# Attention and 7x7 involution on one core: shifted copies become a ring of padded rows, products take 3 or 4 taps, units begin with their own rows, the last two chunks go in half blocks

## The chip, the cores and the metric

The kernel runs on one core of a Trainium2 chip. The metric is the device time of one execution in microseconds (us); less is better. The core has five engines that each work through a queue of their own: TensorE (PE in the profile; its weight loads are shown as PEld), VectorE (DVE), ScalarE (ACT), GpSimd (POOL) and SyncE (SP), which here only issues DMA transfers. They meet through semaphores: an instruction at the head of a queue waits until its semaphores have the value that it needs, and everything behind it in that queue waits too.

## The reference

Everything is float32. `x` is 4 images of 512 channels and 64 x 64 pixels. Layer 0 is self-attention over the 4096 pixels of an image with 128 inner channels; layer 1 is a bottleneck whose middle is an involution: each pixel makes its own 7 x 7 weights for 8 groups of 16 channels.

```python
def _L0_conv_ref(x, wq, bq, wk, bk, wv, bv, wo, bo):
    ...
    q = jnp.einsum('oc,bcn->bon', wq, xf) + bq[:, None]
    k = jnp.einsum('oc,bcn->bon', wk, xf) + bk[:, None]
    v = jnp.einsum('oc,bcn->bon', wv, xf) + bv[:, None]
    energy = jnp.einsum('bci,bcj->bij', q, k)
    attn = jax.nn.softmax(energy, axis=-1)
    out = jnp.einsum('bcj,bij->bci', v, attn)
    out = jnp.einsum('oc,bcn->bon', wo, out) + bo[:, None]
    out = out.reshape(b, c, h, w) + x
    return out
...
def involution(x, Wr, sr, br, Ws, bs):
    w = jax.nn.relu(affine(conv1x1(x, Wr), sr, br))
    w = conv1x1(w, Ws) + bs[None, :, None, None]
    w = w.reshape(B, G, K * K, H, W)
    ...
    out = jnp.einsum('bgkhw,bgckhw->bgchw', w, patches)
    return out.reshape(B, C, H, W)
out = jax.nn.relu(affine(conv1x1(x, W1), s1, b1))
out = involution(out, Wr, sr, br, Ws, bs)
out = affine(conv1x1(out, W3), s3, b3)
return out + x
```

## The kernel before

The whole work is in `fast_path`. (A slower general path follows it, and is entered only if the softmax sums left a safe range; here it is not.) An image is 8 chunks of 512 pixels, a chunk is 8 image rows, and a *unit* of the involution is 4 rows, so 256 pixels: partitions hold 128 pixels, and two such tiles make a unit. An image has 16 units.

*Main line.* For each image `keys_values` (L335) computes the keys `k` and the transposed values `v` chunk by chunk, and `attention` (L481) then runs 32 steps for each chunk of queries. A step is: a score matmul `pss` (128 keys x 512 queries, into one of two PSUM buffers with the tag `s`, L493), an exp on ScalarE into `pt` (L496, five buffers), a matmul `po` with the values (L517), and on VectorE the running sum of the exps `pacc` (L520, L522, at the end `sums`, L525). The score of step m+2 is written ahead of the `po` of step m. Only the last chunk of the last image goes in two half blocks of 256 queries, with 32 steps each.

*Side work.* After each step `chores` (L210) advances three lists of Python generators by a little, so that their instructions fall between those of the main line; the scheduler then sets the final order within each engine's queue. `finish_block` (L388) takes a chunk from the softmax division to layer 1's input: the sum over partitions `pl` (L405), reciprocals (L411), `on` (L414), the projection `pwo` (L418) with the residual (L420), the bottleneck `p1` (L428), its transposed pixels into a padded DRAM image `pix` (L456), and the reduced channels `red` (L465). `close_chunk` (L319) computes the last projection `py` with the residual and writes the output. `pace` (L180) lets the involution go on by 0.78 products for each planned us of TensorE.

*Involution.* A unit is released (L470) when the rows that it needs, three of the next chunk among them, are there. `pump` (L188) then loads its shifted copies from `pix` by four DMA transfers (L204): for 4 and for 3 horizontal shifts, 9 rows each, 1152 and 864 KB, into the pools `sa` (two buffers) and `sb` (one). `weights` (L216) makes the per-pixel weights `pw` of the unit in PSUM, a tile of two banks with a pool tag of its own (L218). `involution` (L230) issues the products: VectorE multiplies two vertical taps at a time, 128 x 512 (L264; 24 of them a unit, and one of a single tap), reading `copies` from SBUF and `pw` from PSUM; POOL adds each product into `acc` (L285) and folds `acc` at the end (L294). There are seven product buffers. `turn_unit` (L298) transposes the sum (`pa`, L308).

*Tail.* After the last image's attention (loop at L542) the units that are left are finished: every second product is then summed by TensorE into `accp` (L279) instead of by POOL, and VectorE adds that sum into `acc` (L293).

PSUM is eight banks of 512 float32 columns a partition. Before, they are: tag `mm` 2, tag `s` 2, `w` (the `pw` tile) 2, `po` 1, `acc` 1.

Of the kernel before, what the change touches and what calls it, by code (L numbers as in the profile page):

```python
# [49 lines left out]
NU = H // UR  # L50
SR = UR + K - 2
WP = W + 2 * PAD
SHIFTS = (0, 4), (4, 3)
TAPS_A_US = 0.78
# [5 lines left out]
COPY_US, X_US, PIX_US, LAND_US = (5.9, 4.4), 3.8, 1.5, 3.0  # L60
# [6 lines left out]
def fast_path(  # L67
# [18 lines left out]

    nc = tc.nc
# [8 lines left out]
    sapool = pool("sa", 2)  # L96
    sbpool = pool("sb", 1)
# [3 lines left out]
    prods = pool("prods", 7)  # L101
    scratch = pool("scratch", 1, space=bass.MemoryType.DRAM)
    ps = pool("ps", 2, space=bass.MemoryType.PSUM)
    ps1 = pool("ps1", 1, space=bass.MemoryType.PSUM)

# [5 lines left out]
    zero = const.tile([WP, PAD, P], F32, name="zero")  # L111
    pix = [
# [16 lines left out]
    begun = {b: 0 for b in range(B)}  # L129
    pending, loaded = [], {}  # L130
    spare = [2, 1]
# [48 lines left out]
    def pace():  # L180
        nonlocal due, seen
        due, seen = min(due + TAPS_A_US * (pe - seen), 10), pe
        for _ in range(2):
            if due < 1 or not step(taps, 1):
                break
            due -= 1

    def pump():  # L188
        for task in list(pending):
            b, u, part, written = task  # L190
            if not spare[part]:
                continue
            pending.remove(task)
            spare[part] -= 1
            dx, n = SHIFTS[part]
            copies = (sapool, sbpool)[part].tile(
                [P, SR, n, P], F32, tag="s", name=f"copies_{b}_{u}_{part}"
            )
            for h in range(2):
                rows = pix[b % 2][UR * u + h : UR * u + h + SR, dx : dx + W, :]  # L200
                windows = bass.AP(
                    tensor=rows.tensor, offset=rows.offset, ap=[[P, W], [WP * P, SR], [1, n * P]]
                )
                nc.sync.dma_start(  # L204
                    copies[h * W : (h + 1) * W].rearrange("p r x c -> p r (x c)"), windows
                )
            free["dma"] = max(free["dma"], written)
            loaded[b, u, part] = copies, takes("dma", COPY_US[part]) + LAND_US
# [5 lines left out]


    def weights(b, u):  # L216
        red, col = reds[b, u]
        pw = ps1.tile([P, NT, CH], F32, tag="w", name=f"pw_{b}_{u}")  # L218
        for t in range(NT):

            rows = slice(t * (P // NT), t * (P // NT) + CR + 1)
            pixels = slice(col + t * P, col + (t + 1) * P)
            mm(
                pw[:, t, : NTAP * G], red[rows, pixels], wt[rows, O_WT : O_WT + NTAP * G],
                shared=2,
            )
        return pw


    def involution():  # L230
        while True:
            while not units:
                yield "none"
            b, u = units.pop(0)
            acc = work2.tile([P, NT, 2, P], F32, tag="acc", name=f"acc_{b}_{u}")
            yield from until(free["dve"] + 0.3)
            pw = weights(b, u)
            begin = pe + 0.5
            first, accp = True, None
            for part, (dx0, nx) in enumerate(SHIFTS):  # L240
                copies, landed = loaded.pop((b, u, part))

                ops = [(x, dy, 2, x * (K - 1) + dy) for x in range(nx) for dy in range(0, K - 1, 2)]
                ops += [(x, K - 1, min(2, nx - x), nx * (K - 1) + x) for x in range(0, nx, 2)]
                for o, (x, dy, n, tap) in enumerate(ops):
                    while not tail and (
                        pe < max(begin, landed)
                        or free["dve"] > pe + 3.5
                        or free["pool"] > pe + 7.5
                    ):  # L250
                        yield "wait"
                    free["pool"] = max(free["pool"], takes("dve", DVE_OP * n / 2))
                    takes("pool", POOL_OP * n / 2)
                    prod = acc
                    if not first:
                        prod = prods.tile(
                            [P, NT, 2, P], F32, tag="prod", name=f"prod_{b}_{u}_{part}_{o}"
                        )
                    col = (dx0 * K + tap) * G
                    if dy < K - 1:  # L260
                        image = copies[:, dy : dy + UR, x, :].rearrange("p (t d) c -> p t d c", t=NT)
                    else:
                        image = copies[:, dy : dy + UR - 1 : 2, x : x + n, :]
                    nc.vector.tensor_tensor(  # L264
                        prod[:, :, :n, :].rearrange("p t d (g c) -> p t d g c", g=G),
                        image.rearrange("p t d (g c) -> p t d g c", g=G),
                        pw[:, :, col : col + n * G].unsqueeze(3)
                        .broadcast_to([P, NT, n * G, GC])
                        .rearrange("p t (d g) c -> p t d g c", d=n),
                        ALU.mult,  # L270
                    )
                    if tail and o % 2:

                        begin_sum = accp is None
                        if begin_sum:
                            accp = ps1.tile(
                                [P, NT, 2, P], F32, tag=("po", "acc")[u % 2], name=f"accp_{b}_{u}"
                            )
                        mm(  # L279
                            accp.rearrange("p t d c -> p (t d c)"), ident,  # L280
                            prod.rearrange("p t d c -> p (t d c)"),
                            begin_sum, part == 1 and o == len(ops) - 2,
                        )
                    elif not first:
                        nc.gpsimd.tensor_tensor(  # L285
                            acc[:, :, :n, :], acc[:, :, :n, :], prod[:, :, :n, :], ALU.add
                        )
                    first = False
                    yield
                spare[part] += 1  # L290
                pump()
            if accp is not None:
                nc.vector.tensor_tensor(acc, accp, acc, ALU.add)  # L293
            nc.gpsimd.tensor_tensor(acc[:, :, 0, :], acc[:, :, 0, :], acc[:, :, 1, :], ALU.add)  # L294
            closing.append(turn_unit(b, u, acc, takes("pool", POOL_OP / 2)))


    def turn_unit(b, u, acc, done):  # L298
        c, i = divmod(u, 2)
        yield from until(done + 2.0)  # L300
        for _ in range(12 if tail else 0):
            yield
        last = (b, c) == (B - 1, NCH - 1)
        if last or i == 0:
            sums_c[b, c] = work1.tile([P, CH], F32, tag="accT", name=f"accT_{b}_{c}")
        pa = ps.tile([P, NT, P], F32, tag="mm", name=f"pa_{b}_{u}")
        for t in range(NT):
            nc.tensor.transpose(pa[:, t, :], acc[:, t, 0, :], ident)  # L308
        pe_us(0.25)
        n = NT * P  # L310
        nc.scalar.copy(sums_c[b, c][:, i * n : (i + 1) * n], pa.rearrange("p t c -> p (t c)"))  # L311
        yield
        if last:
            closing.append(close_chunk(b, c, i * n, n, sums_c.pop((b, c))))
        elif i:
# [19 lines left out]
    def keys_values(b):  # L335
# [11 lines left out]
        for c in range(NCH):  # L347
# [10 lines left out]
            pk = ps.tile([P, CH], F32, tag="s", name=f"pk_{b}_{c}")  # L358
# [29 lines left out]
    def finish_block(b, c, off, n, po, sums):  # L388
# [16 lines left out]
        mm(pl, ones, sums)  # L405
        rl = work1.tile([P, CH], F32, tag="rl", name=f"rl_{name}")[:, :n]
        for i in range(n // P):
            yield
# [7 lines left out]
        for t in range(CT):  # L416
# [6 lines left out]
            yield  # L423
            if t != 1 and not late:
                yield
        p1 = ps.tile([P, CH], F32, tag="mm", name=f"p1_{name}")[:, :n]
        for t in range(CT):
            mm(p1, w_slice(O_W1, t), xt[:, t, :], t == 0, t == CT - 1)  # L428
            if t == 1:
# [31 lines left out]
        written = takes("dma", PIX_US) + LAND_US  # L461
# [8 lines left out]
        while begun[b] < NU and (begun[b] * UR + UR + PAD <= rows or rows == H):  # L470
            u = begun[b]
            begun[b] += 1
            pending.extend((b, u, part, written) for part in range(2))
            units.append((b, u))
# [6 lines left out]
    def attention(b, kt, vT):  # L481
        nj = N // P
        blocks = [(c, 0, CH) for c in range(NCH)]
        if b == B - 1:

            blocks[-1:] = [(NCH - 1, off, CH // 2) for off in (0, CH // 2)]
# [3 lines left out]
        def score(m):  # L490
            k, j = divmod(m, nj)
            n = blocks[k][2]
            pss = ps.tile([P, CH], F32, tag="s", name=f"pss_{b}_{k}_{j}")[:, :n]  # L493
            mm(pss, kt[:, j * P : (j + 1) * P], qs[k])
            pt = ptpool.tile([P, CH], F32, tag="pt", name=f"pt_{b}_{k}_{j}")[:, :n]
# [5 lines left out]
        for m in range(len(blocks) * nj):  # L501
            k, j = divmod(m, nj)
            c, off, n = blocks[k]
            if j == 0:
                pos[k] = ps1.tile([P, CH], F32, tag="po", name=f"po_{b}_{k}")[:, :n]
                paccs[k] = ps1.tile([P, CH], F32, tag="acc", name=f"pacc_{b}_{k}")[:, :n]
# [7 lines left out]
            if m + 2 < len(blocks) * nj:  # L514
                score(m + 2)
            pt = pts.pop(m)
            mm(pos[k], vT[:, j, :], pt, j == 0, j == nj - 1)  # L517
            takes("dve", DVE_OP * n / CH)
# [4 lines left out]
            else:  # L523
                sums = work1.tile([P, CH], F32, tag="sums", name=f"sums_{b}_{k}")[:, :n]
# [435 lines left out]
```

## Time and profile before

| what | value |
|---|---|
| median of 3 runs | 2763.79 us (2763.5 to 2765.86) |
| the profiled execution | 2762.84 us |
| its span in the trace | 2761.0 us |
| TensorE matmuls | 2679.7 us busy, 97% |
| VectorE | 1951.8 us, 71% |
| POOL | 1892.8 us, 69% |
| ScalarE | 894.5 us, 32% |
| DMA | 377.78 MB, mean 137 GB/s |
| transfers `copies<-pix` | 128 of 1152 KB, landing 13.4 us after issue; 128 of 864 KB, 14.3 us |
| scores `pss` (L168) | 2112 records, 1055.5 us busy, 0.0 us idle before them |
| first matmul | 10.84 us after the start |

A 512-column float32 matmul shows as two records of 0.43 us. `mm` (L166) is the helper through which nearly all matmuls go, so they are told apart by their tiles, not by line. A row of groups reads: line, engine, operation, output and inputs with their shapes, count, then busy us and mean ns of one, then the idle time of that engine just before them and what ended it. A row of windows gives busy us and instructions of PE, PEld, DVE, ACT and POOL in a stretch, the granted TensorE clock (1.00 is full), the share of the DMA engines' time in use and GB/s.

### The profile page before, as it was taken

Reading aid. Unit: us, or ns where it says so; the run is one execution under the profiler, and the core shown is the slowest. Engines: PE = TensorE matmul, PEld = TensorE weight load, DVE = VectorE, ACT = ScalarE, POOL = GpSimd, SP = SyncE. Lnnn points to the kernel's source line nnn. Section 1 sums busy time; section 2 is a strip of 40 time slices with the busy share of each in tenths; the row PEclk is TensorE's granted clock in tenths of the full one; section 3 lists DMA queues with packets and bytes.
Section 4 is the critical chain, followed back from the end, with each engine's and each line's share of the span. In section 5 each row is a group of like instructions: output and inputs, shape, how many; then the busy total and the mean of one; then the engine's idle time right before and its main releaser. Section 6 shows DMA issues by size and latency. Waiting matters only on the chain.

```text
span 2761.0 us, 24223 instructions
## 1 busy us (share of the span) xinstructions
PE 2679.7 (97%) x6694; PEld 1205.4 (44%) x6694; DVE 1951.8 (71%) x3091; ACT 894.5 (32%) x1514; POOL 1892.8 (69%) x1548
## 2 busy tenths in 40 slices
PE   8999999999899999999999999999989999999986
PEld 4444444444344444444444444444434444444742
DVE  0356888786586678777566687788747758787886
ACT  2333333332233333333233333333323333333410
POOL 0004887788785478778876477787877548787875
PEclk9999999999999999999999999999999999999998
DMA  6033566668844567766863367766894445666695
GB/s 238 16 64 71 115 144 146 144 136 219 176 113 95 108 145 154 154 141 139 207 158 81 84 114 151 154 136 147 185 227 120 110 88 119 140 143 130 143 195 124
DMA packets 223057, 377.78 MB, mean 137 GB/s; under 512 B 7928, under 2 KB 100288, under 8 KB 222784
## 3 DMA queue, kind: packets, MB, share of 16 engines
q1 hardware_dynamic: 222624, 374.74, 61.6%
q8 instruction: 54, 0.88, 0.1%
q10 hardware_dynamic: 288, 1.42, 0.1%
q14 instruction: 91, 0.75, 0.1%
HBM read 333.29 MB, written 42.77 MB: 136 GB/s over the span
## 4 chain that ended last, share of the span: by engine, by line
PE 91%; DVE 3%; POOL 3%; DMA 1%; issue 0%; ACT 0%; POOLq 0%; SPq 0%; DVEq 0%; ACTq 0%
PE pss L168 32%; PE po L168 32%; PE p L168 4%; PE pq L168 4%; PE py L168 4%; PE pwo L168 4%; PE pk L168 3%; PE pv L168 3%; POOL acc L285 3%; DVE prod L264 2%; PE pw L168 2%; PE pl L168 1%; PE pr L168 1%; PE accp L168 1%; PE pa L308 1%; DMA copies<-pix 1%
## 5 line engine op out<-in xcount | busy, mean ns | idle before, releaser
L285 POOL TENSOR_TENSOR acc<-acc,prod 128x512 f32<-128x512 f32 x1476 | 1844.9, 1250 | 843.8 <-DVE prod L264 538.0
L168 PE MATMUL pss<-q,k 128*128 128x512 f32 (+1 forms) x2112 | 1055.5, 582 | 0.0
L168 PE MATMUL po<-pt,v 128*128 128x512 f32 (+1 forms) x2112 | 1052.4, 580 | 0.0
L264 DVE TENSOR_TENSOR prod<-copies,pw 128x512 f32<-128x512 f32 (+1 forms) x1536 | 974.0, 670 | 89.2 <-POOL acc L285 79.5
L496 ACT ACTIVATE pt<-pss 128x512 f32<-128x512 f32 (+1 forms) x1056 | 616.5, 584 | 1213.7 <-PE pss L168 1080.0
L522 DVE TENSOR_TENSOR pacc<-pacc,pt 128x512 f32<-128x512 f32 (+1 forms) x990 | 672.5, 679 | 451.5 <-ACT pt L496 443.1
L168 PEld LDWEIGHTS po<-pt,v 128*128 128x128 f32 x2112 | 399.6, 190 | 480.8 <-issue 464.4
L168 PEld LDWEIGHTS pss<-q,k 128*128 128x128 f32 x2112 | 393.6, 190 | 466.4 <-issue 455.0
L168 PE MATMUL pwo<-on,wt 128*128 128x512 f32 (+1 forms) x264 | 131.6, 584 | 5.2 <-DVE xb L420 5.2
L168 PE MATMUL py<-accT,wt 128*128 128x512 f32 (+1 forms) x264 | 134.0, 596 | 2.0 <-ACT accT L311 2.0
L168 PE MATMUL pq<-xb,wt 128*128 128x512 f32 (+1 forms) x264 | 120.4, 600 | 8.2 <-DVE xb L326 8.2
L411 DVE RECIPROCAL rl<-pl 128x128 f32<-128x128 f32 x128 | 118.6, 941 | 12.6 <-PE pl L168 12.6
L168 PE MATMUL p<-xb,wt 128*128 128x512 f32 (+1 forms) x264 | 123.3, 593 | 2.4 <-DVE xb L420 2.4
L437 ACT ACTIVATE xb<-xb,vec 128x512 f32<-128x512 f32 (+1 forms) x132 | 93.0, 707 | 98.8 <-PE p L168 94.4
L168 PE MATMUL pk<-xa,wt 128*128 128x512 f32 x256 | 123.4, 623 | 0.3 <-DMA xa<-x_dram 0.3
L168 PE MATMUL pv<-xa,wt 128*128 128x512 f32 x256 | 116.1, 593 | 0.0
L326 DVE SCALAR_TENSOR_TENSOR xb<-py,vec,xb 128x512 f32<-128x512 f32 (+1 forms) x132 | 96.3, 732 | 20.5 <-PE py L168 20.2
L420 DVE SCALAR_TENSOR_TENSOR xb<-pwo,bo,xb 128x512 f32<-128x512 f32 (+1 forms) x132 | 96.2, 732 | 19.7 <-PE pwo L168 19.2
L264 DVE TENSOR_TENSOR acc<-copies,pw 128x512 f32<-128x512 f32 x64 | 43.4, 678 | 89.0 <-PE pw L168 88.9
L520 DVE COPY pacc<-pt 128x512 f32<-128x512 f32 (+1 forms) x33 | 22.3, 677 | 88.5 <-ACT pt L496 88.5
L168 PEld LDWEIGHTS pq<-xb,wt 128*128 128x128 f32 x264 | 51.4, 197 | 68.2 <-issue 54.0
L168 PEld LDWEIGHTS p<-xb,wt 128*128 128x128 f32 x264 | 51.2, 195 | 64.5 <-issue 55.3
(49 smaller groups left out, 875.0 us busy)
## 6 DMA issues: line engine op xcount, KB each, us to landing
copies<-pix SPq DMA_DIRECT2D x128, 1152.0 KB, 13.4
copies<-pix SPq DMA_DIRECT2D x128, 864.0 KB, 14.3
xa<-x_dram SPq DMA_DIRECT2D x32, 1024.0 KB, 11.8
xb<-x_dram SPq DMA_DIRECT2D x32, 1024.0 KB, 6.0
out_dram<-xb SPq DMA_DIRECT2D x31, 1024.0 KB, 9.6
pix<-o1t SPq DMA_DIRECT2D x62, 128.0 KB, 2.5
wt<-wts_dram ACTq DMA_DIRECT2D x1, 1284.0 KB
out_dram<-xb SPq DMA_DIRECT2D x2, 512.0 KB, 3.5
```

The lines of the kernel that those rows point to most:

```text
L168: nc.tensor.matmul(o, lhsT=lhsT, rhs=rhs, start=start, stop=stop)
L264: nc.vector.tensor_tensor(prod[:, :, :n, :].rearrange("p t d (g c) -> p t d g c", g=G), image.rearrange("p t d (g c) -> p t d g c", g=G), ...
L285: nc.gpsimd.tensor_tensor(acc[:, :, :n, :], acc[:, :, :n, :], prod[:, :, :n, :], ALU.add)
L308: nc.tensor.transpose(pa[:, t, :], acc[:, t, 0, :], ident)
L326: nc.vector.scalar_tensor_tensor(xt[:, t, :], py, v1(V_S3 + t), xt[:, t, :], ALU.mult, ALU.add)
L411: nc.vector.reciprocal(rl[:, cols], pl[:, cols])
L420: nc.vector.scalar_tensor_tensor(xt[:, t, :], pw, bo[:, t : t + 1], xt[:, t, :], ALU.add, ALU.add)
L437: nc.scalar.activation(xt[:, t, :], xt[:, t, :], AF.Identity, bias=v1(V_B3 + t))
L496: nc.scalar.activation(pt, pss, AF.Exp)
L520: nc.vector.tensor_copy(paccs[k], pt)
L522: nc.vector.tensor_tensor(paccs[k], paccs[k], pt, ALU.add)
```

## The change

1. *Ring.* The pools `sa` and `sb` are gone. `ring` is one SBUF tile of 12 padded rows that holds each row at its 7 horizontal shifts. `pump` loads rows that have not been loaded yet, as many as are written, have room, and fit before the ring's end; the row of image b with number r has the place (72 b + r) mod 12.
2. *Products* take 4 vertical taps (dy 0 to 3) or 3 (dy 4 to 6) of one horizontal shift; where the rows pass the ring's end a product is split into 2 + 2 or 2 + 1. Of three units in a row one has 14 products and two have 21. `acc` and the product buffers are four taps wide (before, two); there are four product buffers (before, seven). POOL folds `acc` in two steps, 512 and 256 columns.
3. *Release.* A unit is put on the list with its own rows; its second half (dy 4 to 6) waits until its rows are loaded.
4. *PSUM.* One tile `banks` of four banks takes the place of the two `s` buffers and of the `w` tile: banks 0 and 1 in turn for scores and `pk` (`score_bank`), banks 2 and 3 for `pw`. In the tail `pw` takes banks 0, 1 and 2, 3 in turn, and that of the next unit is made halfway through a unit (`early`).
5. *Half blocks.* In the last image the last two chunks go in halves (before, the last one), with 16 steps of two key blocks each, so that an exp is 512 wide; `pl` is then two matmuls into one sum.
6. *Tail.* `accp` is summed in pieces of two taps; ScalarE copies it to `accs`, and the fold and the transposition are done by 12 small matmuls into `pa`. `turn_unit` waits 7 turns, not 12. `finish_block` yields less in the last two chunks.

```diff
-    sapool = pool("sa", 2)
-    sbpool = pool("sb", 1)
...
-    prods = pool("prods", 7)
+    prods = pool("prods", 4)
...
+    banks = ps1.tile([P, 2 + NT, CH], F32, name="banks")
...
+    ring = const.tile([P, RING, K, P], F32, name="ring")
...
     def pump():
...
+        nonlocal load
+        while load // STEP in written:
+            b, row = divmod(load, STEP)
+            rows, us = written[b]
+            end = H + SR - UR if rows == H else rows + PAD - 1
+            n = min(b * STEP + end, low + RING) - load
+            n = min(n, RING - load % RING)
+            if n <= 0:
+                break
             for h in range(2):
...
+                src = pix[b % 2][row + h : row + h + n, :W, :]
                 windows = bass.AP(
...
+                    tensor=src.tensor, offset=src.offset, ap=[[P, W], [WP * P, n], [1, K * P]]
                 )
...
+    def score_bank():
+        turns[0] = 1 - turns[0]
+        return banks[:, turns[0]]
     def weights(b, u):
...
-        pw = ps1.tile([P, NT, CH], F32, tag="w", name=f"pw_{b}_{u}")
+        turns[1] = 2 - turns[1] if tail else 2
+        pw = banks[:, turns[1] : turns[1] + NT]
...
     def involution():
...
+            pw = early.pop((b, u), None) or weights(b, u)
...
+            for dy0, n in DYS:
+                at = (base + dy0) % RING
+                whole = at + n + NT < RING + 1
+                pieces = [(dy0, n)] if whole else [(dy0, 2), (dy0 + 2, n - 2)]
+                ops += [(x, dy, k) for x in range(K) for dy, k in pieces]
...
+                if o and dy >= DYS[1][0] > ops[o - 1][1]:
+                    low = base + UR
+                    pump()
+                    if tail and units:
+                        early[units[0]] = weights(*units[0])
...
+                while base + dy + n + NT > load:
+                    yield "wait"
...
+                for n in (2, 1):
+                    nc.gpsimd.tensor_tensor(
+                        acc[:, :, :n, :], acc[:, :, :n, :], acc[:, :, n : 2 * n, :], ALU.add
+                    )
...
     def turn_unit(b, u, acc, accp, done):
...
+            accs = work1.tile([P, CH // P, P], F32, tag="o1t", name=f"accs_{b}_{u}")
+            nc.scalar.copy(accs, accp.rearrange("p t d c -> p (t d) c"))
+            for t in range(NT):
+                parts = [acc[:, t, d, :] for d in range(4)] + [accs[:, 2 * t + d, :] for d in range(2)]
+                for i, part in enumerate(parts):
+                    mm(pa[:, t, :], part, ident, i == 0, i == len(parts) - 1)
...
-            pk = ps.tile([P, CH], F32, tag="s", name=f"pk_{b}_{c}")
+            pk = score_bank()
...
-        while begun[b] < NU and (begun[b] * UR + UR + PAD <= rows or rows == H):
...
+        written[b] = rows, us
+        units.extend((b, u) for u in range(top // UR, rows // UR))
         pump()
...
-            blocks[-1:] = [(NCH - 1, off, CH // 2) for off in (0, CH // 2)]
+            blocks[-2:] = [(c, off, CH // 2) for c in (NCH - 2, NCH - 1) for off in (0, CH // 2)]
...
-            pss = ps.tile([P, CH], F32, tag="s", name=f"pss_{b}_{k}_{j}")[:, :n]
-            mm(pss, kt[:, j * P : (j + 1) * P], qs[k])
+            pss = score_bank()
+            for i in range(CH // n):
+                key = (j * (CH // n) + i) * P
+                mm(pss[:, i * n : (i + 1) * n], kt[:, key : key + P], qs[k])
```

## The prediction

> **What bounds the kernel now.** I read the busy table and the slices first.
>
> ```profile
> PE 2679.7 (97%) x6694; PEld 1205.4 (44%) x6694; DVE 1951.8 (71%) x3091; ACT 894.5 (32%) x1514; POOL 1892.8 (69%) x1548
> ...
> PEclk9999999999999999999999999999999999999998
> ...
> PE 91%; DVE 3%; POOL 3%; DMA 1%; issue 0%; ACT 0%; POOLq 0%; SPq 0%; DVEq 0%; ACTq 0%
> ```
>
> TensorE is busy in nearly the whole span, at full clock, and is 91% of the chain that ended last. So a gain can come only from work taken off TensorE or from its few gaps, and every new wait of TensorE costs its full length. The windows show where the gaps lie (columns: window; span, busy us and instructions of PE, PEld, DVE, ACT, POOL; clock; DMA share; GB/s):
>
> ```profile
> 633.65:730.13 96.48, 83.42 (x220) 37.01 (x218) 54.70 (x84) 20.95 (x35) 84.30 (x70) 0.95 0.91 221
> 730.00:1295.00 565.00, 564.99 (x1377) 248.57 (x1376) 427.77 (x673) 200.27 (x333) 404.56 (x329) 1.00 0.59 127
> 2635.00:2761.00 126.00, 93.33 (x209) 37.30 (x208) 93.09 (x157) 5.81 (x14) 81.55 (x69) 0.85 0.72 151
> ```
>
> An attention stretch (730 to 1295) has no gap at all. A change of image (633.65 to 730.13, and two like it) has gaps, and so has the tail. The timeline of the attention loop shows the pattern that matters here:
>
> ```profile
> 1001.01 1.02 PE L168 MATMUL pss<-q,k 128*128 128x512 f32 x2
> 1001.87 1.02 PE L168 MATMUL po<-pt,v 128*128 128x512 f32 x2
> 1002.07 0.60 ACT L496 ACTIVATE pt<-pss 128x512 f32<-128x512 f32 x1 [1.12 <-PE pss L168]
> 1002.70 0.70 DVE L522 TENSOR_TENSOR pacc<-pacc,pt 128x512 f32<-128x512 f32 x1 [1.02 <-ACT pt L496]
> 1002.73 1.02 PE L168 MATMUL pss<-q,k 128*128 128x512 f32 x2
> ```
>
> A step is one score and one `po`, 0.86 us of TensorE each (two records of 0.43; starts lie 0.86 apart). The score shown as 1.02 ends 0.16 after its last issue; its exp starts 0.04 later and takes 0.60. The next score starts at 1002.73, before anything has to be ready but the exp of two scores back. The score banks are a rotating pair of their own, and `pw` is another tile.
>
> **Accounts of before.** The profiled run took 2762.84, 0.95 under the median of 2763.79: span 2761.0 and 1.84 outside it. First matmul at 10.8; matmuls up to the last `po` counted at 0.86 for each 512 columns, 2550.8; changes of image 96.5, 97.7 and 97.5 long with 77.6 of matmuls in each, so 59 lost; the tail from 2635, 126; the rest, 14.3, is small gaps.
>
> **The change: what decides.** `banks` makes one PSUM tile of the two score banks and the two `pw` banks. I followed the waits in the compiled program of the new kernel. Accesses by different engines to that tile are ordered one after the other, though they lie in different banks. Of the 1088 score matmuls, 627 wait for a DVE product that reads `pw` and that itself waits for the exp of the score just before; most others wait for that exp. In the old program a score waits only for the exp of two scores back, and a product only for POOL and DMA. So where products run, score, exp, product and next score are now one serial loop. The `po` between two scores mostly reads the exp just made too, so it lies beside the product, not beside the exp.
>
> Price of a loop: 0.16 (end of score) + 0.04 + 0.60 (exp) + 0.04 (hop; the trace has 1002.67 to 1002.70) + product D + 0.04 + 0.10 (a matmul after a wait is shown 1.12 long, not 1.02), so 0.98 + D, against the matmuls W between the scores. D comes from two groups of the same instruction:
>
> ```profile
> L264 DVE TENSOR_TENSOR prod<-copies,pw 128x512 f32<-128x512 f32 x1472 | 948.4, 681 | 80.6 <-POOL acc L285 71.2 <-DMA copies<-pix 4.8 <-PE accp L168 1.1
> L264 DVE TENSOR_TENSOR prod<-copies,pw 128x256 f32<-128x256 f32 x64 | 26.6, 416 | 8.7 <-POOL acc L285 8.3
> ...
> 2644.88 11.17 DVE L264 TENSOR_TENSOR prod<-copies,pw 128x512 f32<-128x512 f32 x19
> L496 ACT ACTIVATE pt<-pss 128x512 f32<-128x512 f32 x992 | 592.0, 597 | 1174.4 <-PE pss L168 1044.7 <-DVE xb L420 57.4 <-DVE pacc L522 35.2
> ```
>
> One tap more is 0.265; in a row a product is 11.17/19 = 0.588, so 0.06 + 0.265 a tap, and 0.09 more standing alone. Four taps 1.21, three 0.95, 2+2 1.29, two products of four 2.3. Counted over the new program's score-to-score intervals (TensorE idle each, times number):
> - product of D about 1.03, only a `po` of 0.86 between, which itself follows the exp: 0.98 + 1.03 - 0.86 = 1.15, 248 times: 288
> - two products (D 1.96), one `po` between: 2.08, 69 times: 143
> - product, W about 1.7: 0.33, 57 times, 19; 1.4, 17 times, 23
> - product, W over 1.8: 236 times, together 46 (0.12 where the first matmul of 0.86 ends before the exp, about 0.5 for two products)
> - exp only, two scores in a row: 0.97, 90 times: 88; with 0.86 before the waiting matmul 0.12, 251 times: 30
> Sum about 640. In 186 intervals DVE work queued ahead of the product (pacc 0.70, reciprocal 0.94, STT 0.75) ends after the exp; the excess adds 155, of which 65 falls beside the key/value phases, where no score waits: 90. Together **730**. Low bound: no hop, no restart (0.76 + D) gives 480, and 60 for the queued DVE work: 540. High: hops of 0.06 and a restart of 0.2 (1.12 + D) give 770, and 130: 900.
>
> The Trainium skill, PSUM — Partial Sum Buffer, section "PSUM bank collisions raise a hardware error", asks for semaphores by bank and quadrant and says that different banks run clean. By that rule none of these waits is needed and the sum would be the first rival's, 2728; the program sets them all the same.
>
> **The other parts.**
> - Ring: a row of 459 KB is loaded once, 276 rows, 127 MB, instead of 64 units x 4.03 MB = 258 MB; SP issues 311 transfers, not 368. In attention the DMA share was 0.59 and hides behind TensorE: nothing. A ring load waits on SP for the products that read the rows it overwrites; behind it on SP stand the `xa`, `xb`, pix and output transfers, and `pk` would wait for `xa`. So it can cost only at the changes of image.
> - Products of 3 or 4 taps: on average 18.7 a unit, not 25; DVE 49 x 0.265 + 18.7 x 0.06 = 14.1 us a unit. POOL (1.273 for 512, 0.73 for 256, so about 2.36 and 1.82 for 4 and 3 taps) 28.9 a unit with the wider folds, not 30.7. A unit has about 53 us in 3450, so POOL hides. Four product buffers wait for the sum four back, hidden for the same reason.
> - Units with their own rows and less DMA: the changes of image have POOL busy 84 of 97 us and DMA 0.91. Products start earlier, loads are halved; but six `pk` matmuls and 27 more now wait for a product of about 1 us in these phases. I take 45 for the three, not 59; bounds 15 (POOL full) and 100 (each of 33 waits costs 1.2 and nothing is gained).
> - Half blocks: the extra `pl` matmul columns 1.7, and smaller changes: TensorE 2553.1 up to the last `po`.
> - Tail: four units (12 to 15) instead of five: products 4 x 14.1 = 57, other DVE 17, start 2, waits 10, and the 17 that ran from the last product to the end before: 103 instead of 126, with bounds 95 and 115. A transfer of copies, 15.06 us on the tail's chain, goes, since the ring holds the rows. There an ACT copy and 12 small matmuls a unit stand for a DVE add (0.70) and a POOL fold (0.73): counted in the 10.
>
> Sum: 10.8 + 2553.1 + 14.3 + 730 + 45 + 103 + 1.8 = **3458**. I say 3450. Own range: with all lows 10.8 + 2553.1 + 14.3 + 540 + 15 + 95 + 1.8 = 3230; with all highs, 900, 100 and 115: 3695.
>
> **The rivals.**
> - *The loop does not bind* (the other side). Place: score to score in attention. If exp and product were done before TensorE comes to the next score, the 730 are nothing: 3458 - 730 = 2728, faster by 35 (14 at the changes of image, 23 in the tail, less 2.3 of matmuls). It decides from W of 2.0 (0.98 + 1.03) on. For it: the hardware has slack in ACT (32%) and DVE (71%). Against: W is 0.86 in 317 of the 627, and the order in the queues is fixed. 6%.
> - *Products run ahead of the exp*, so that only their own length and the DVE work before them binds, about 250: 2728 + 250 = 2978. Against: 624 products have the wait for the exp. 7%.
> - *The clock falls in the stalled stretches.* TensorE would be busy some 60% of them. In the tail the clock row of the slices falls in the last slice, and a window of the tail at 0.85; after a gap of 2.73 us eight `pq` matmuls took 5.30 instead of 3.44, while after gaps of 1.74 eight `p` matmuls took 3.70. If all 480 stalled scores took 1.72, +413: 3870; half of them: 3660. 12%. The Trainium skill, TensorE: Matmul & The Clock Gate, Part 1, names an idle window of about 3.4 us, longer than the gaps seen here; by it this rival gives nothing, 3458.
>
> **How the numbers follow.** Forecast 75%, rivals 6, 7 and 12%. The likeliest is 3450; the range reaches from the all-lows sum a little down and, for the lower half of the clock rival, to 3710; outside are the first two rivals (13%) and half of the third (6%). This kernel can't tell less than 0.2% (5.5 us; its runs lie 2.4 apart) from no change. Faster 0.06, same 0.01 (a partial loop that just eats the 35), slower 0.93.
>
> **What would show it.** In the new profile: idle time of `pss` matmuls put down to DVE products and to exps, several hundred us where it was 0.0; PE share near 78%; scores some 2.9 to 3.1 us apart where products run; products waiting for ACT. DMA near 247 MB; a tail near 100. I am wrong if scores stay 1.72 apart while products run.

## The result

The changed kernel takes 3518.18 us (median of 4 runs, 3510.8 to 3520.65) against 2764.82 us of the kernel before: 1.272 times as long (95% interval 1.269 to 1.274). The profiled execution took 3510.8 us, with a span of 3508.5 us. The page of the changed kernel, its busy table, three of the rows of slices and the two groups that answer to the old `pss` and product rows:

```profile
PE 2999.6 (85%) x6932; PEld 1150.3 (33%) x6932; DVE 1968.1 (56%) x2635; ACT 893.1 (25%) x1495; POOL 1816.2 (52%) x1187
...
PE   8998878888889887888989888888897988888878
...
PEclk9999999999999999999999999999999999999999
DMA  5040222224304112222521321122260222211323
...
L177 PE MATMUL banks<-q,k 128*128 128x512 f32 (+1 forms) x2176 | 1157.8, 619 | 185.2 <-DVE prod L301 118.7
L301 DVE TENSOR_TENSOR prod<-ring,banks 128x512 f32<-128x512 f32 (+3 forms) x1092 | 897.0, 852 | 736.3 <-ACT pt L548 603.0
```

VectorE does fewer and wider products in 897 us instead of 974, and the DMA engines move 240 MB instead of 378; both were meant. But VectorE now sits idle ahead of products for 603 us until an exp is done, scores wait for products, and TensorE is no longer busy throughout. The waits of TensorE over the whole run (engine, tile and line, what it waited for; us in total, times, longest):

```profile
PE po L177 <- ACT pt L548: 236.2, 326, 1.0
PE banks L177 <- DVE prod L301: 119.0, 180, 2.9
PE banks L177 <- ACT pt L548: 62.7, 88, 0.7
PE pa L351 <- POOL acc L334: 46.0, 22, 2.8
```

These sum to some 460 us, and the kernel lost 753. The rest hides in the busy column: matmuls drain for 0.16 us and start anew when the stream breaks, and both are shown as busy, which is why TensorE is "busy" 320 us longer for nearly the same matmul work (2549 and 2551 us up to the last `po`). To see the whole loss I took the start times of the matmul records: the distance of each to the next, less its work (0.43 us for 512 columns):

| us | before | changed |
|---|---|---|
| matmul work up to the last `po` | 2549 | 2551 |
| lost in attention, clock full | 17 | 766 |
| lost in attention to half clock | 0 | 64 |
| lost in the three changes of image | 59 | 20 |
| from the last `po` to the end | 126.2 | 97.6 |

A piece of the timeline of the changed kernel shows the loop (start and length in us; in brackets the idle time before and what ended it):

```profile
1423.69 1.12 PE L177 MATMUL banks<-q,k 128*128 128x512 f32 x2 [0.80 <-DVE prod L301]
1424.91 0.60 ACT L548 ACTIVATE pt<-banks 128x512 f32<-128x512 f32 x1 [3.20 <-PE banks L177]
1425.56 1.12 PE L177 MATMUL po<-pt,v 128*128 128x512 f32 x2 [0.75 <-ACT pt L548]
1425.61 0.95 DVE L301 TENSOR_TENSOR prod<-ring,banks 128x768 f32<-128x768 f32 x1 [1.37 <-ACT pt L548]
1426.48 0.69 DVE L579 TENSOR_TENSOR pacc<-pacc,pt 128x512 f32<-128x512 f32 x1
1426.62 1.12 PE L177 MATMUL banks<-q,k 128*128 128x512 f32 x2
1427.78 0.60 ACT L548 ACTIVATE pt<-banks 128x512 f32<-128x512 f32 x1 [2.27 <-PE banks L177]
1428.43 1.12 PE L177 MATMUL po<-pt,v 128*128 128x512 f32 x2 [0.69 <-ACT pt L548]
1428.48 0.95 DVE L301 TENSOR_TENSOR prod<-ring,banks 128x768 f32<-128x768 f32 x1 [1.31 <-ACT pt L548]
1429.49 1.13 PE L177 MATMUL banks<-q,k 128*128 128x512 f32 x2
```

Read it downwards: score, exp, then `po` and the product side by side, then the next score 2.87 us after the last (1429.49 - 1426.62), 0.06 after the product's end at 1429.43; the predicted interval was 1.72 + 1.15 = 2.87. Before, the same two matmuls came every 1.72 us.

### The profile page after: what moved, and what is told of

Same layout as the page of the kernel before. It is cut to its first block, busy times and chain, and to the rows that moved or that the text cites. A ratio compares the mean times of both kernels' runs of the same rounds, so it can differ in the third digit from the quotient of the medians.

```text
span 3508.5 us, 22755 instructions
## 1 busy us (share of the span) xinstructions
PE 2999.6 (85%) x6932; PEld 1150.3 (33%) x6932; DVE 1968.1 (56%) x2635; ACT 893.1 (25%) x1495; POOL 1816.2 (52%) x1187
## 5 line engine op out<-in xcount | busy, mean ns | idle before, releaser
L325 POOL TENSOR_TENSOR acc<-acc,prod 128x768 f32<-128x768 f32 (+3 forms) x1059 | 1695.7, 1610 | 1668.1 <-DVE prod L301 1636.6
L177 PE MATMUL po<-pt,v 128*128 128x512 f32 (+1 forms) x2176 | 1122.5, 610 | 236.5 <-ACT pt L548 236.2
L177 PE MATMUL banks<-q,k 128*128 128x512 f32 (+1 forms) x2176 | 1157.8, 619 | 185.2 <-DVE prod L301 118.7
L301 DVE TENSOR_TENSOR prod<-ring,banks 128x512 f32<-128x512 f32 (+3 forms) x1092 | 897.0, 852 | 736.3 <-ACT pt L548 603.0
L548 ACT ACTIVATE pt<-banks 128x512 f32<-128x512 f32 x1024 | 611.3, 597 | 2052.4 <-PE banks L177 2049.4
L579 DVE TENSOR_TENSOR pacc<-pacc,pt 128x512 f32<-128x512 f32 x956 | 664.6, 695 | 440.9 <-ACT pt L548 440.7
L177 PEld LDWEIGHTS banks<-q,k 128*128 128x128 f32 x2176 | 360.3, 193 | 881.2 <-DVE prod L301 481.5
L301 DVE TENSOR_TENSOR acc<-ring,banks 128x1024 f32<-128x1024 f32 (+1 forms) x84 | 79.2, 962 | 155.8 <-ACT pt L548 135.1
L177 PE MATMUL pwo<-on,wt 128*128 128x512 f32 (+1 forms) x272 | 136.2, 587 | 13.9 <-DVE on L467 13.9
L177 PE MATMUL banks<-xa,wt 128*128 128x512 f32 x256 | 125.2, 622 | 0.6 <-DVE prod L301 0.3
L334 POOL TENSOR_TENSOR acc<-acc 128x512 f32<-128x512 f32 x120 | 119.4, 995 | 9.4
```

The lines of the kernel that those rows point to most:

```text
L177: nc.tensor.matmul(o, lhsT=lhsT, rhs=rhs, start=start, stop=stop)
L301: nc.vector.tensor_tensor(prod[:, :, p0 : p0 + n, :].rearrange("p t d (g c) -> p t d g c", g=G), image.rearrange("p t d (g c) -> p t d g c ...
L325: nc.gpsimd.tensor_tensor(acc[:, :, d0 : d0 + n, :], acc[:, :, d0 : d0 + n, :], prod[:, :, :n, :], ALU.add,)
L334: nc.gpsimd.tensor_tensor(acc[:, :, :n, :], acc[:, :, :n, :], acc[:, :, n : 2 * n, :], ALU.add)
L548: nc.scalar.activation(pt, pss, AF.Exp)
L579: nc.vector.tensor_tensor(paccs[k], paccs[k], pt, ALU.add)
```

## The experiments

All times are medians, compared with the kernel before run on the same chip.

**The sharing alone taken back** (`e1_separate`).

```diff
-    banks = ps1.tile([P, 2 + NT, CH], F32, name="banks")
...
     def score_bank():
-        turns[0] = 1 - turns[0]
-        return banks[:, turns[0]]
+        turns[0] += 1
+        return ps.tile([P, CH], F32, tag="s", name=f"score_{turns[0]}")
...
-        turns[1] = 2 - turns[1] if tail else 2
-        pw = banks[:, turns[1] : turns[1] + NT]
+        pw = ps1.tile([P, NT, CH], F32, tag="w", name=f"pw_{b}_{u}")
...
-                    if tail and units:
-                        early[units[0]] = weights(*units[0])
```

> The changed kernel with the PSUM sharing alone taken back: scores in the rotating pair with tag s, pw in a tile of its own, and pw of the next unit in the tail made when that unit starts. Theory (the shared tile makes the loop score, exp, product, score): all but about 0 of the 766 us of idle TensorE in attention and the 64 us at half clock go, so 3515 - 830 = 2685 plus some 17 of small gaps as before and up to 10 in the tail for the pw that is no longer made early: 2695 to 2730, faster than before by 1 to 2.5%. Rival (the ring, the wide products or the earlier release make the stalls): it stays above 3200.

Measured: 2694.02 us, 0.9747 (0.973 to 0.9763) of before. The one edit takes away 824 us, and what is left of the change is a gain. The busy table of its page, and a piece of its timeline:

```profile
PE 2653.7 (99%) x6932; PEld 1237.2 (46%) x6932; DVE 1909.5 (71%) x2635; ACT 894.8 (33%) x1495; POOL 1818.3 (68%) x1187
```

```profile
1002.46 1.02 PE L176 MATMUL score<-q,k 128*128 128x512 f32 x2
1002.80 0.90 DVE L297 TENSOR_TENSOR prod<-ring,pw 128x768 f32<-128x768 f32 x1
1003.31 1.02 PE L176 MATMUL po<-pt,v 128*128 128x512 f32 x2
1004.17 1.02 PE L176 MATMUL score<-q,k 128*128 128x512 f32 x2
```

TensorE is busy 99%, and scores are 1.71 us apart again with a product between them. The same holds over the whole run. Of the intervals from one score to the next with one `po` between them and a full clock, the changed kernel has 175 of 1.7 or 1.8 us, and a product starts in none of them; in `e1_separate` all 591 are 1.7 or 1.8 us long, and products start in 275. Lost in attention by the start times: 20 us at full clock, none at half. So the 766 and the 64 both came from the shared tile, and neither the ring nor the wide products had a part in them.

**The sharing alone put into the kernel before** (`e2_before_shared`): one tile of four banks for `pk`, `pss` and `pw`.

```diff
+    banks = ps1.tile([P, 2 + NT, CH], F32, name="banks")
...
-        pw = ps1.tile([P, NT, CH], F32, tag="w", name=f"pw_{b}_{u}")
+        pw = banks[:, 2:]
...
-            pk = ps.tile([P, CH], F32, tag="s", name=f"pk_{b}_{c}")
+            pk = score_bank()
...
-            pss = ps.tile([P, CH], F32, tag="s", name=f"pss_{b}_{k}_{j}")[:, :n]
+            pss = score_bank()[:, :n]
```

> The kernel before with the sharing alone put in: scores, pk and pw in one PSUM tile of four banks, all else as before. Theory: 762 products wait for the exp just issued and 767 scores for a product; with 0.98 us for the hops and the exp, and 1.09 us of products on average against 1.37 us of matmuls between, some 690 us of idle, 90 for DVE work queued ahead and 60 at half clock come on top of 2765: about 3600, range 3400 to 3750. Rival (the stalls come from the new ring and products): within 2% of 2765.

Measured: 3547.13 us, 1.2831 (1.281 to 1.2853). By the start times attention lost 809 us at full clock, 792 more than before (the estimate was 690 + 90 = 780), and 46 at half clock (60). The sum was 50 too high for another reason: the changes of image lose 7 us instead of 59. 2765 + 792 + 46 - 52 = 3551. Why they lose less is not shown. The units are not further ahead: when a change begins, 258 of the image's 784 taps are still to come, 256 in the kernel before. But only 98 taps fall into the change, where it was 137, and no `pa` waits for POOL there. The same loop stands in this kernel's timeline with two-tap products (x2: two of them in a row):

```profile
1358.27 1.12 PE L170 MATMUL banks<-q,k 128*128 128x512 f32 x2 [0.26 <-DVE prod L270]
1359.49 0.60 ACT L502 ACTIVATE pt<-banks 128x512 f32<-128x512 f32 x1 [2.66 <-PE banks L170]
1360.14 1.13 PE L170 MATMUL po<-pt,v 128*128 128x512 f32 x2 [0.75 <-ACT pt L502]
1360.19 1.28 DVE L270 TENSOR_TENSOR prod<-copies,banks 128x512 f32<-128x512 f32 x2 [1.36 <-ACT pt L502]
1361.53 1.13 PE L170 MATMUL banks<-q,k 128*128 128x512 f32 x2 [0.26 <-DVE prod L270]
```

The products at 1360.19 waited for an exp, and the score at 1361.53 starts 0.06 after they are done at 1361.47; the two scores are 3.26 us apart instead of 1.72.

**Which pair of users costs it** (`e3_pair_shared`): the score pair stays one tile, `pw` gets its own.

```diff
-    banks = ps1.tile([P, 2 + NT, CH], F32, name="banks")
+    pair = ps1.tile([P, 2, CH], F32, name="pair")
+    wpair = ps1.tile([P, NT, CH], F32, name="wpair")
...
-        return banks[:, turns[0]]
+        return pair[:, turns[0]]
...
-        pw = banks[:, turns[1] : turns[1] + NT]
+        pw = (pair, None, wpair)[turns[1]]
```

> The changed kernel with pw in a PSUM tile of its own, while the two score banks still are one tile (in the tail pw takes the two tiles in turn, as in the changed kernel). Theory: products wait no more for an exp; a score waits for the exp just before it, which costs 0.97 us where two scores stand in a row and 0.12 otherwise, about 80 us: 2690 + 80 = 2770, range 2720 to 2850. Rival (the pair of score banks is the larger part of the coupling): above 3000.

Measured: 2745.62 us, 0.9932 (0.9915 to 0.9948). Attention lost 80 us, 59 more than with separate tiles. So `pw` beside the scores is nearly all of the price, 766 - 80 = 686, and the pair of scores the rest.

**What the other parts are worth.** Each of these starts from the kernel with separate tiles and takes one thing back or puts one in.

```diff
 (e4_old_release)
-        units.extend((b, u) for u in range(top // UR, rows // UR))
+        while begun[b] < NU and (begun[b] * UR + UR + PAD <= rows or rows == H):
+            units.append((b, begun[b]))
+            begun[b] += 1
 (e5_one_halved)
-            blocks[-2:] = [(c, off, CH // 2) for c in (NCH - 2, NCH - 1) for off in (0, CH // 2)]
+            blocks[-1:] = [(NCH - 1, off, CH // 2) for off in (0, CH // 2)]
 (e6_two_taps)
-    prods = pool("prods", 4)
+    prods = pool("prods", 7)
...
-                pieces = [(dy0, n)] if whole else [(dy0, 2), (dy0 + 2, n - 2)]
+                pieces = [(dy0, 2), (dy0 + 2, n - 2)]
...
-                        [P, NT, 4, P], F32, tag="prod", name=f"prod_{b}_{u}_{o}"
+                        [P, NT, 2, P], F32, tag="prod", name=f"prod_{b}_{u}_{o}"
 (e7_early, the tail's second pw in a pool opened when the scores' pool is closed)
+    scoring.close()
+    spare.append(pool("spare", 1, space=bass.MemoryType.PSUM))
...
+                    if tail and units:
+                        early[units[0]] = weights(*units[0])
```

> Separate PSUM tiles (as in e1_separate, 2694), and units released as in the kernel before, when three halo rows of the next chunk are there. If the earlier release is what shortened the changes of image and left four units for the tail instead of five, about 20 us come back in the tail (one unit more at 14.1 of products, 9 at least for the rest of the chain) and up to 15 at the changes of image: 2705 to 2730. Rival (the ring alone did it, units could not start earlier anyway since their second half waits for the same rows): within 0.2% of 2694.

Measured: 2694.31 us, 0.9737 (0.9722 to 0.9752), no difference from `e1_separate` that can be told. The earlier release is worth nothing here: the rival holds. So this run also serves as the measure for the next three, which ran on the same chip.

> As e1_separate, but only the last chunk of the last image goes in half blocks (so without the second part of the change's half blocks). The half blocks of the last chunk but one bring two units forward by up to a quarter of a chunk (15 us); if the tail is bound by the units' products, the tail grows by 5 to 20: 2697 to 2714. Rival: the units wait for POOL and VectorE anyway: within 0.2% of 2694.

Measured: 2697.25 us, 2.9 more than `e4_old_release`, at the low edge of what was expected; 0.9747 (0.9732 to 0.9761) of the kernel before, which can't be told from `e1_separate`. What the halves of the last chunk but one bring is 3 us at most, or nothing. In the profiled executions the tail is 6.9 us longer without them (101.3 against 94.4 from the last `po` to the end), and 1.6 us of that come back ahead of the last `po`.

> As e1_separate, but every product is split in 2 + 2 or 2 + 1 taps as at the ring's end, with seven narrow buffers. VectorE then needs 16 us a unit instead of 14, POOL 30.7 instead of 28.9. In attention neither binds; in the tail four units of 2 us more each, and at the changes of image some 2 to 5 each for POOL: 2694 + 8 + 10 = 2712, range 2700 to 2725. Rival (the width of the products is worth nothing, the gain of e1_separate is all ring and release): within 0.2% of 2694.

Measured: 2715.67 us, 21.4 more than `e4_old_release`; 0.9813 (0.9798 to 0.9828). The size was about right, the place was not: at the changes of image this kernel lost under 2 us in all, less than `e1_separate` (14), while the time from the last `po` to the end grew from 94.5 to 135.7. The windows of that stretch, first of `e1_separate`, then of `e6_two_taps` (span, busy us and instructions of PE, PEld, DVE, ACT, POOL; clock; DMA share; GB/s):

```profile
2595.30:2689.80 94.50, 78.17 (x280) 42.12 (x279) 72.65 (x97) 7.78 (x17) 58.72 (x37) 0.97 0.34 84
```

```profile
2578.70:2714.40 135.70, 105.62 (x374) 63.19 (x372) 98.99 (x185) 9.71 (x21) 94.35 (x75) 0.89 0.36 91
```

With narrow products VectorE has 99 us of work there instead of 73: some of the involution is put off to the tail, where it lies open. After the last `po` start 154 products with 266 taps, where `e1_separate` has 70 with 196; at 49 taps a unit that is 5.4 units instead of 4.

> As e1_separate, with the part of the tail that it left out put back: the pool of the score pair is closed before the tail, and pw of the next unit is made there halfway through a unit. e3_pair_shared, which kept it, ran 89.5 us from the last po to the end, e1_separate 94.4: so 2694 - 5 = 2689, range 2684 to 2694. Rival: the next pw is not on the tail's chain: no difference from 2694.

Measured: 2690.12 us, 0.9721 (0.9707 to 0.9734): 4.2 less than `e4_old_release`; the time from the last `po` to the end is 90.3, against 94.5 in `e1_separate`.

**The tail's fold, and the pace.**

```diff
 (e8_old_fold)
+            if accp is not None:
+                nc.vector.tensor_tensor(acc[:, :, :2, :], accp, acc[:, :, :2, :], ALU.add)
+                accp = None
...
-        for _ in range(7 if tail else 0):
+        for _ in range(12 if tail else 0):
 (e9_faster_pace)
-TAPS_A_US = 1.56
+TAPS_A_US = 1.72
```

> As e7_early (2690), but with the tail's fold of the kernel before: VectorE adds accp into acc (0.70), POOL folds 512 and 256 columns (1.27 and 0.73), two transposes, 12 turns of waiting. If the fold by 12 small matmuls shortens the tail, some 2 us for each of four units, one of them surely on the chain, come back: 2692 to 2702. Rival (the fold lies beside other work for all but the last unit, and is 1 us there): within 0.2% of 2690.

Measured: 2702.7 us (2700.3 to 2703.38), 12.6 more than `e7_early`, more than expected. All of it lies in the tail: from the last `po` to the end this kernel takes 102.8 us, `e7_early` 90.3. The 12 turns of waiting instead of 7 went in with the old fold, and neither was tried alone, so the 12.6 belong to the two together.

> As e7_early, with 1.72 taps for each planned us of TensorE in place of 1.56. If products wait for their turn in attention and units so pile up for the tail and for the changes of image, 3 to 10 us go: 2680 to 2687. Rival (units wait for their rows, not for their turn): within 0.2% of 2690, or slower by up to 10 as POOL's queue gets in the way of other work.

Measured: 2689.98 us, no difference. So the pace is not what holds units back here.

The fastest kernel, `e7_early`, is some 75 us under the one before (77 by the runs on the same chip, 2690.12 against 2767.01). Wide products make about 21 of it, the fold with the shorter wait 13, the early `pw` 4, the halves 0 to 3, the release nothing. The remaining 36 or so are left for the ring and the smaller edits that went in with it; none of that was run alone, so it is a remainder, not a measured part.

## Why the prediction was right

*The loop* was the step that mattered: 730 was forecast, 766 less the 17 of small gaps that there were before, 749, was measured, and `e1_separate` and `e2_before_shared` put it on the shared tile from both sides. The row arithmetic held for the common intervals: of 447 with one `po` between two scores and full clock, 175 had no product and were 1.7 or 1.8 us long, 135 were 2.9 or 3.0, and 51, with two products, 3.7 to 4.3; 2.87 and 3.80 had been worked out. But that the total came so close is in part luck. Of the 749, by the starts, 44 stand before `pa`, which waits for POOL's fold, and 14 before `pwo`, which waits for `on` (the profile puts 1.9 and 2.9 there in the whole of `e1_separate`). The sum had both at nothing, since POOL was to hide behind TensorE; the loop alone took some 690.

*The changes of image* were mis-sized: 45 was taken, 20 was lost. The bound of 100, a full wait for each of the key matmuls, was far off; the few that waited cost little, since with separate tiles the three lose 14, 6 less. And `e2_before_shared` shows that the sharing alone, with the old products and the old release, brings them from 59 to 7, which the sum did not count.

*The tail* was forecast at 103 from the last `po` to the end and took 97.6.

*The clock* was a rival at 12%, at 413 us if every stalled score ran at half rate. It came true in a small part: 64 us. That term, taken as nothing in the sum, is the largest miss. The forecast of 3458 plus 64, less 25 and 5, plus 19 for the waits in attention, is 3511; the profiled execution took 3510.8. So no large term is missing, but the misses partly cancelled: two terms were 83 us too small together, two others 30 too large.

*The first two rivals* fell. The loop binds, since the matmuls between two scores are too few, and products did wait for the exp just issued (603 us). But the price of the first rival, 2728 for everything but the loop, was in turn too high: with the loop gone the kernel ran 2694, for 31 fewer at the changes of image and 8 fewer in the tail.

*What would show it*: idle time of scores put down to products and exps, and products waiting for ACT, were there; the PE share was 85%, not 78, because a matmul after a wait is shown longer (1.12) and with its drain, and at half clock still longer (2.07). DMA moved 240 MB, where 247 were forecast: the 258 MB of the old copies had been added up from KB of 1024 bytes and are 264.

The Trainium skill, PSUM — Partial Sum Buffer, section "PSUM bank collisions raise a hardware error", was weighed in the prediction: different banks run clean. The runs agree that nothing in the chip asked for the waits: the same accesses, to different banks but in tiles of their own, ran 824 us faster. The waits were set by the program, which orders the users of one tile.

## What to carry to other kernels

Give each PSUM buffer a tile of its own, above all where different pairs of engines work on them, even where one larger tile is handier: the banks may be apart, but here waits were set by the tile. Before a change goes to the chip, look in the compiled program at what the matmuls of the critical engine wait for; a wait for an engine that was never there before is worth more attention than any saving. And read lost time on TensorE from the starts of matmuls, not from the busy share, which counts drains and restarts as work.

## What was not expected of the hardware

The clock of TensorE fell to half in stretches of attention though no gap between matmuls there was longer than 3.05 us. Windows of the changed kernel around the drop at 1245.5:

```profile
1238.70:1242.10 3.40, 3.31 (x10) 1.23 (x8) 1.31 (x2) 0.97 (x2) 0.00 (x0) 1.00 0.00 0
1242.10:1245.50 3.40, 1.55 (x3) 0.59 (x4) 2.03 (x3) 0.60 (x1) 2.21 (x1) 0.99 0.00 0
1245.50:1248.90 3.40, 2.69 (x4) 0.50 (x2) 2.59 (x3) 0.00 (x0) 2.49 (x2) 0.50 0.00 0
```

In the window ahead of the drop TensorE was busy 1.55 of 3.40 us, with gaps between matmuls of 1.4 and 1.0 us by their starts. The Trainium skill, TensorE: Matmul & The Clock Gate, Part 1, ties the half clock to an idle window of about 3.4 us; here it came after a window that was only half idle.

Another stalled window of the same run kept the full clock (with the one behind it):

```profile
713.00:716.40 3.40, 1.71 (x5) 0.39 (x3) 3.40 (x5) 0.60 (x1) 3.08 (x3) 1.00 0.00 0
716.40:719.80 3.40, 2.62 (x5) 0.81 (x6) 3.40 (x4) 0.60 (x1) 2.77 (x2) 1.00 0.01 1
```

What decided can be read from the starts. The 30 stretches of half clock in this run begin whole multiples of 3.413 us apart. Cut on that grid, each window gets the matmul work that falls into it (0.43 us for each 512-column record, so without drains): 1.23 us in the window ahead of the drop above, 1.30 in the one that kept its clock. I did this for seven of the traces (`before`, `after`, `e1_separate`, `e2_before_shared`, `e3_pair_shared`, `e6_two_taps` and `e7_early`), from 80 us on. Each has such a grid. The 82 windows ahead of a drop hold at most 1.35 us of work, and the 5653 others that ran at full clock hold at least 1.27; 20 windows lie between these two. So in these runs the clock fell where matmuls filled less than about 38% of a window, however the gaps lay in it.

`on`, a VectorE product of two SBUF operands of 128x512, took 893 ns before, 1164 in `e7_early` and 1730 in the changed kernel, while products that read one operand from PSUM kept their time (942 and 946 ns for 3 taps with separate and shared tiles). TensorE waited 13.9 us for it. The traces show what it waited for:

```profile
149.69 0.68 DVE L467 TENSOR_TENSOR on<-on,rl 128x512 f32<-128x512 f32 x1
...
2141.70 1.80 POOL L325 TENSOR_TENSOR acc<-acc,prod 128x768 f32<-128x768 f32 x1 [0.25 <-DVE prod L301]
2142.07 1.99 DVE L467 TENSOR_TENSOR on<-on,rl 128x512 f32<-128x512 f32 x1
```

At 149.69 POOL was idle, and `on` took 0.68 us. At 2142.07 POOL was in the middle of an instruction that ended at 2143.50, and `on` ended at 2144.06, 0.55 to 0.56 later. In `before`, `after`, `e1_separate`, `e2_before_shared` and `e7_early` it was so each time: 47 of these `on` (128x512) started beside an idle POOL and took 0.67 to 0.69 us, and 105 started during a POOL instruction and ended 0.55 us after it. In the changed kernel 28 of 30 started so, in the kernel before 11 of 31, and POOL's instructions are now up to 2.35 us long where they were 1.27.
